# Second half of a two-layer network: all engines in program order, routing in single slots, another answer path for group 0, a weighted fill of the last slots

## The chip, the core and the metric

The program runs on one core of one Trainium2 chip. A core has a matrix engine (TensorE, PE in the profile, with its weight loads as PEld), a vector engine (VectorE, DVE), a scalar engine (ScalarE, ACT), GpSimd (POOL) and SyncE (SP), which here only issues DMAs. Every engine works through its own list of instructions in the order in which the list was written; semaphores tie the lists together. The metric is the time of one execution on the device in microseconds (us), lower is better.

## The reference

The input is 2048 rows of 128 numbers (8 sequences of 256). Four blocks follow one another, each with a residual and a layer norm. The last one is what the change is about.

```python
x = layernorm(x + attention0(x))      # 16 heads, Taylor features, causal
x = layernorm(x + ffn0(x))            # two routed experts and a shared one
x = layernorm(x + attention1(x))      # 16 heads of 8, rotary, causal softmax
x = layernorm(x + ffn1(x))            # 8 experts, each row goes to its best 2

scores = x @ Wg.T                                     # 8 scores a row
topk_scores, topk_idx = top_k(scores, 2)
topk_probs = softmax(topk_scores)
hidden = silu(x @ W1[e].T) * (x @ W2[e].T)            # 256 wide
expert_out = hidden @ W3[e].T
out = sum over the two chosen e of topk_prob * expert_out
```

## The kernel before, in words

Rows are worked in NG = 4 **groups** of 512 rows (2 sequences, TG = 4 tiles of 128). The first half of the program (layer 0's attention, and ffn0 of group 0) lies under a block in which PE, ACT, DVE and SP all keep the order of the program text. The second half, `second_half()`, is the rest: ffn0 of groups 1 to 3, attention 1 and the expert block. It lies under a block that keeps the program's order for PE alone. The order of the lists of ACT, DVE, POOL and SP is made there by a planner, which places each instruction by its own model of costs.

`second_half()` runs over **slots** s = -14, -13, ... Six slots belong to a sequence b. In a slot the text emits, in this order: the attention's score maxima (`largest`, even slots) or its softmax weights (`weights`, odd slots); the pieces that were fixed to this slot with `at(s, ...)`; n pieces from `queue`; and a quarter of `attend1` for the sequence before. Up to slot FREE = 24 the queue holds the pieces of ffn0. From then on it holds the expert work of the groups in turn. LATE = 54 is the first slot after the last sequence's attention, LAST = 68 the slot by which the queue is to be empty: between the two, n is the number of pieces left over the slots left.

The **expert block of a group g** goes so. `back1`, `ended1` and `normed1` finish attention and its layer norm (`spreads` has DVE, then an ACT square root, then DVE). `routed` then fixes these steps to slots: `turn` (transposes), `scores` and `ranks`, `count` and `places` (where each row goes), `chances` (the softmax of two). `sent` scatters the rows, two indirect DMAs of POOL for each tile of 128 rows, into the DRAM tensor `slots`, in which each of SN = 15 tiles of 128 places belongs to one expert. `begun` calls `networks`, which asks for the first rows and expert weights (`rows` and `weights`, DMAs of SP) and puts 27 pieces into the queue: 4 `turn_in` (transposes of 4 tiles), 15 `up` (8 matmul passes for one tile; from LATE on two tiles at once), 8 `down` (second matmul of two tiles). `joined` brings the answers back, in one of two ways:

- **gathered** (groups 0, 1 and 2): `down` copies a pair of tiles with ACT and stores it with one DMA of SP to `answers`; when all are there, POOL gathers with 8 indirect DMAs (line 1417), DVE adds the two weighted answers (`summed`, lines 1428 and 1431), then the norm (`spread`) and the output (`stored`).
- **scattered** (group 3): the row carries its weight and its destination as two more columns (`pay`, SW = 130), so `down` scales each tile at once (DVE line 1376, ACT line 1378) and scatters it with an indirect DMA of POOL to the row's own place (line 1381, 15 in all); then 4 direct DMAs load it (`loaded`), and DVE adds (`added`).

All work of `up` in a slot from LATE on uses two double banks of PSUM in turn; its silu is ACT line 1335, its product DVE line 1336. [...]

Slots of importance, before: group 0, 1, 2, 3 start their expert work in slot 34, 46, 58, 67. For group 3: `back1` of its last sequence in slot 56, `ended1` 57, `normed1` 58, `turn` 59, `scores` 60, `count` 61, `placed` 62, `chances` 63, `sent` 64 and 65, `begun` 67.

Of the kernel before, what the change touches and what calls it, by code (L numbers as in the profile page):

```python
# [11 lines left out]
F32 = mybir.dt.float32  # L12
# [6 lines left out]
P = 128  # L19
B, T, D = 8, 256, 128  # L20
NT = B * T // P
TG = 4
NG = NT // TG
GW = TG * P
# [5 lines left out]
E, F = 8, 256  # L30
NFC = E * F // P
SN = 2 * TG + E - 1
SW = D + 2
SC = 3 * P
NEG = -1e30
# [44 lines left out]
def network(  # L80
# [22 lines left out]
    dram = ctx.enter_context(tc.tile_pool(name="dram", bufs=1, space=bass.MemoryType.DRAM))  # L103
# [88 lines left out]
    for j in range(4):  # L192
# [6 lines left out]
        out=before,  # L199
# [9 lines left out]


    slots = [
        dram.tile([SN * P, SW if g == NG - 1 else D], F32, tag=f"slots{g}", name=f"slots{g}")
        for g in range(NG)
    ]
    answers = [
        dram.tile(
            [2 * GW if g == NG - 1 else SN * P, D], F32, tag=f"answers{g}", name=f"answers{g}"
        )
        for g in range(NG)
    ]  # L220
# [486 lines left out]
    def second_half():  # L707
# [5 lines left out]
        def at(s, *piece):  # L713
            fixed.setdefault(s, []).append(piece)
# [255 lines left out]
        def ended1(b):  # L970
            g, s = b // 2, b % 2
            yT = yTs.pop(b)
            po = bank(f"pz_{b}")
            for q in range(2):
                nc.tensor.matmul(
                    po[:, q * P : (q + 1) * P],
                    yT[:, q * P : (q + 1) * P],
                    wo1_sb,
                    start=True,
                    stop=True,  # L980
                )
            if s == 0:
                rs[g] = gpool.tile([P, TG, D], F32, tag="r", name=f"r2_{g}")
            nc.vector.tensor_add(
                rs[g][:, 2 * s : 2 * s + 2, :],
                po[:, : 2 * P].rearrange("p (q d) -> p q d", q=2),
                xs[g][:, 2 * s : 2 * s + 2, :],
            )
            if s == 1:
                at(6 * (b + 2) + 4, normed1, g, spreads(rs[g], f"b{g}"))  # L990

        def normed1(g, spread):
            pay = None
            if g == NG - 1:
                pay = [
                    route.tile([P, TG, SW], F32, tag=f"pay{r}", name=f"pay{g}{r}", bufs=1)
                    for r in range(2)
                ]
                xs[g] = scaled_rows(rs[g], f"b{g}", spread, pay[0][:, :, 0:D])
                nc.scalar.copy(pay[1][:, :, 0:D], xs[g])  # L1000
            else:
                xs[g] = scaled_rows(rs[g], f"b{g}", spread)
            routed(g, pay, 12 * g + 22)


        nets = {}

        def routed(g, pay, s):

            turn, scores, chances, count, places = gates(g, xs[g], pay)  # L1010

            def placed():
                slot_is[g], nets[g] = places()

            late = g == NG - 1
            for i, piece in zip((1, 2, 3, 4, 5) if late else (2, 3, 4, 5, 7), (turn, scores, count, placed, chances)):
                at(s + i, piece)
            for t in range(TG):
                at(s + (6 + t // 2 if late else 8 + t), sent, g, pay, t)
            at(s + (9 if late else 12), begun, g)  # L1020

        def sent(g, pay, t):

# [9 lines left out]
                apart(i, f"slots{g}")  # L1033

        def begun(g):
            queue.extend(networks(g, nets[g]))


        for g in range(NG):
# [1 line left out]
        for b in range(B):  # L1041
            at(6 * (b + 1) + 5, turned, b, 0)
            at(6 * (b + 1) + 5, turned, b, 1)
            at(6 * (b + 2) + 2, back1, b)
            at(6 * (b + 2) + 3, ended1, b)
        queue += in_line(
            [ffn0(g, mid, bank, o_bank, lambda _: slot[0] % 2 == 0) for g in range(1, NG)]
        )
        s = -14
        while s < 6 * B or fixed or queue:  # L1050
            slot[0] = s
            b, k = s // 6, s % 6
            if s == FREE:
                mid_done()
            if s == LATE:
                turns.append(a_bank)
            if 0 <= b < B:
                if k == 0:
                    turn_maxima(b)
            if k % 2 == 0 and 0 <= b + 1 < B:  # L1060
                largest(b + 1, k // 2)
            if k % 2 == 1 and 0 <= b < B:
                weights(b, k // 2)
            for f, *a in fixed.pop(s, ()):
                f(*a)
            n, left = 0, len(queue)
            if s < FREE and left:

                ends = [i for i, f in enumerate(queue) if f[0].__name__ == "normed"]
                n = -(-(ends[0] + 1) // (12 * (NG - len(ends)) - 13 - s))  # L1070
            elif s < LATE:
                n = 2 - s % 2
            elif s < LAST:
                n = -(-left // (LAST - s))
            else:
                n = 6
            while n > 0 and queue:
                f, *a = queue.pop(0)
                n -= f(*a) is not False
            if 1 <= k <= 4 and 0 <= b - 1 < B:  # L1080
                attend1(b - 1, k - 1)
            s += 1
# [175 lines left out]
    def fetch(what, used=0):  # L1258
        spent[what] += used
        while ahead[what] and fetched[what] - spent[what] < {"rows": 2, "weights": 4}[what]:  # L1260
            f, *a = ahead[what].pop(0)
            f(*a)
            fetched[what] += 1

    def networks(g, nets_i):
# [2 lines left out]
        xg, xT, we, hT, di, gs = {}, {}, {}, {}, {}, {}  # L1268
        n_chunks = -(-SN // TG)
        n_pairs = -(-SN // 2)  # L1270
        last = g == NG - 1
        width = SW if last else D

        def net(i, engine):
# [115 lines left out]
            if m == n_pairs - 1:  # L1390
                joined(g)

        ahead["rows"] += [(rows, c) for c in range(n_chunks)]
        ahead["weights"] += [(weights, i) for i in range(SN)]
        fetch("rows")
        fetch("weights")
        out = [(turn_in, 0)]
        for m in range(n_pairs + 2):
# [4 lines left out]
                    out.append((turn_in, m // 2 + 1))  # L1403
            if m - 2 >= 0:
                out.append((down, m - 2))
        return out

    def joined(g):

# [48 lines left out]
        if g == NG - 1:  # L1458
            later(s + 1, begin)
            later(s + 1, loaded)  # L1460
            for h in range(2):
                for f in (added, spread, stored):
                    later(s + 1, f, slice(2 * h, 2 * h + 2))
        elif s < LATE:
            later(s + 3, begin)
            for t in range(TG):
                later(s + 3 + t, gathered, t)
                later(s + 5 + t, summed, t)
            later(s + 9, spread, every)
# [124 lines left out]
```

## Time and profile before

| | |
|---|---|
| median of 3 runs | 610.4 us (609.34 to 612.27) |
| profiled execution: its own time, and its span from the first to the last instruction | 610.17 us, 608.4 us |
| mean granted TensorE clock | 0.938 |
| busy in the span: PE, DVE, ACT, POOL | 86%, 54%, 41%, 28% |
| matmuls of `up` (L1329) and `down` (L1353) | 66.8 us, 35.1 us |
| indirect DMAs of POOL: sends to `slots` (L1025), gathers (L1417), answers of group 3 (L1381) | 32 of 0.97 us, 24 of 0.96 us, 15 of 0.99 us |
| expert weights (L1293), SP | 60 DMAs of 256 KB, 3.3 us to landing |
| slot 54 (LATE) begins, read from the first `up` behind the last attention transposes | 485.1 us |
| first and last matmul of group 3's expert work | 555.9 us, 585.7 us |

Busy time of an engine is the sum of its instructions; an instruction that waits isn't busy, and what it waited for is inferred from semaphores. The difference between an execution's time and its span (1.8 us here) lies outside the instructions. PE's granted clock stands beside the busy digits, in tenths of full speed, for 40 equal slices of 15.2 us.

### The profile page before, as it was taken

To read this page: it belongs to the slowest core of one execution; us is meant where nothing else is said; L and a number is where in the kernel's file an instruction comes from. 1 tells how busy PE (TensorE), PEld (TensorE's weight loads), DVE (VectorE), ACT (ScalarE), POOL (GpSimd) and SP (SyncE) were. 2 spreads that over 40 slices of the span, in tenths; PEclk is the share of its full clock that TensorE was granted. 3 is DMA by queue.
4 is the path that set the end of the run, shared out by engine and by line. 5 is a ranking of instruction groups with operands and counts; after the bars stand their busy time and mean duration, and the time that the engine had idled before them with its cause. 6 is when DMAs were issued, how large, how long until landed. Compare 5 with 4: busy or idle time off the path is not lost.

```text
span 608.4 us, 10761 instructions
## 1 busy us (share of the span) xinstructions
PE 524.0 (86%) x4194; PEld 340.6 (56%) x4194; DVE 327.6 (54%) x759; ACT 248.1 (41%) x367; POOL 170.1 (28%) x208
## 2 busy tenths in 40 slices
PE   5799999999989999899989989899999859748750
PEld 2455656666654544344554546456678659748740
DVE  2346678478565162744564555746955436632424
ACT  2276444636341124144446344345547318322130
POOL 5022212222230030012213112452172540451670
PEclk9799999999999999989999996799999879998785
DMA  9106803230250000000000000231226357729512
GB/s 321 61 1 170 216 19 70 71 72 6 66 141 0 1 0 2 0 2 0 1 1 1 1 1 2 75 100 32 70 94 195 105 154 211 233 82 260 168 41 70
DMA packets 40562, 47.34 MB, mean 78 GB/s; under 512 B 3655, under 2 KB 29404, under 8 KB 39488
## 3 DMA queue, kind: packets, MB, share of 16 engines
q1 hardware_dynamic: 37520, 40.33, 23.8%
q0 software_dynamic: 2560, 5.02, 2.5%
q10 hardware_dynamic: 432, 1.31, 0.6%
q8 instruction: 34, 0.56, 0.4%
q14 instruction: 16, 0.13, 0.1%
HBM read 35.95 MB, written 11.15 MB: 77 GB/s over the span
## 4 chain that ended last, share of the span: by engine, by line
PE 65%; DVE 14%; POOL 6%; DMA 5%; ACT 5%; issue 4%; SPq 1%; POOLq 0%; ACTq 0%; DVEq 0%
PE pf L640 6%; PE pg L1329 6%; PE ph L622 5%; PE pv L356 5%; PE py L436 5%; PE sb L897 4%; PE pd L1353 4%; PE po L516 4%; DVE mx L860 4%; PE sa L828 3%; PE s L397 3%; PE pr L758 3%; POOL yb L1417 2%; PE pa L930 2%; PE py L444 2%
## 5 line engine op out<-in xcount | busy, mean ns | idle before, releaser
L1329 PE MATMUL pg<-xTs,we 128*128 128x128 f32 x480 | 66.8, 293 | 26.7 <-DVE hT L1336 14.5
L1329 PEld LDWEIGHTS pg<-xTs,we 128*128 128x128 f32 x480 | 61.7, 206 | 29.5 <-DVE hT L1336 15.5
L909 POOL TENSOR_SCALAR_AFFINE_SELECT pr<-pr 128x512 f32<-128x512 f32 (+1 forms) x48 | 37.7, 795 | 127.7 <-ACT pr L907 127.4
L460 POOL TENSOR_TENSOR y<-y 128x512 f32<-128x512 f32 x32 | 35.1, 1096 | 135.3 <-DVE y L453 103.4
L860 DVE TENSOR_REDUCE mx<-sa 128x4 f32<-128x1024 f32 (+1 forms) x48 | 56.5, 1219 | 27.3 <-PE sa L851 19.7
L414 DVE SCALAR_TENSOR_TENSOR at<-at,causal 128x1024 f32<-128x1024 f32 x32 | 39.2, 1225 | 42.2 <-ACT at L413 42.0
L413 ACT ACTIVATE at<-s,rt_half 128x1536 f32<-128x1536 f32 x32 | 49.2, 1536 | 17.7 <-PE s L405 17.7
L907 ACT ACTIVATE pr<-sb 128x1024 f32<-128x1024 f32 x48 | 46.5, 1021 | 17.3 <-PE sb L897 17.2
L897 PE MATMUL sb<-qm,kr 32*128 32x128 f32 (+1 forms) x512 | 34.6, 353 | 8.1 <-DVE mx L860 7.9
L436 PE MATMUL py<-at,v 128*64 128x256 f32 x256 | 41.1, 400 | 0.6 <-DVE at L414 0.3
L356 PE MATMUL pv<-wv,xt 128*128 128x512 f32 x64 | 35.3, 652 | 2.1 <-DVE kT L349 1.4
L640 PE MATMUL pf<-hq,w 128*128 128x512 f32 x72 | 37.0, 605 | 0.0
L516 PEld LDWEIGHTS po<-wo_sb,y 128*128 128x128 f32 x256 | 30.8, 192 | 9.6 <-issue 4.2
L1353 PE MATMUL pd<-e,hT 128*128 x240 | 35.1, 292 | 0.6 <-issue 0.3
L897 PEld LDWEIGHTS sb<-qm,kr 32*128 32x128 f32 x512 | 22.8, 189 | 20.1 <-DVE mx L860 17.2
L1417 POOL DMA_INDIRECT yb<-answers,slot_i x24 | 23.0, 960 | 39.4 <-DMA answers<-yg 27.2
L516 PE MATMUL po<-wo_sb,y 128*128 128x128 f32 x256 | 32.1, 278 | 1.9 <-DVE st L471 1.5
L1353 PEld LDWEIGHTS pd<-e,hT 128*128 128x128 f32 x240 | 31.5, 203 | 1.9 <-issue 1.1
L1025 POOL DMA_INDIRECT slots<-x_b,slot_i x24 | 23.3, 971 | 27.9 <-DVE nets L1244 22.2
L1335 ACT ACTIVATE sg<-pg 128x512 f32<-128x512 f32 (+1 forms) x24 | 13.5, 563 | 36.6 <-PE pg L1329 36.5
L930 PE MATMUL pa<-pr,vaug 128*32 128x128 f32 (+1 forms) x512 | 28.3, 338 | 0.0
L634 DVE TENSOR_SCALAR hq<-ph,sml 128x512 f32<-128x512 f32 x20 | 14.9, 749 | 22.7 <-PE ph L622 22.7
(228 smaller groups left out, 932.6 us busy)
## 6 DMA issues: line engine op xcount, KB each, us to landing
we<-in_e SPq DMA_DIRECT2D x60, 256.0 KB, 3.3
bc<-nr SPq DMA_DIRECT2D x14, 512.0 KB, 5.6
slots<-empty SPq DMA_DIRECT2D x3, 960.0 KB, 10.3
answers<-yg SPq DMA_DIRECT2D x21, 128.0 KB, 3.1
xg<-slots SPq DMA_DIRECT2D x9, 256.0 KB, 3.4
w<-in_w SPq DMA_DIRECT2D x2, 768.0 KB, 7.1
xt<-in_xt SPq DMA_DIRECT2D x4, 256.0 KB, 9.3
x<-in_x SPq DMA_DIRECT2D x4, 256.0 KB, 8.8
```

The source lines that it names most:

```text
L356: nc.tensor.matmul(pv, xT[:, t * P : (t + 1) * P], wv_sb[:, w], start=True, stop=True)
L413: nc.scalar.activation(at, ps[:, :, 0:SC], AF.Square, bias=rt_half, scale=SQ_SCALE)
L414: nc.vector.scalar_tensor_tensor(at[:, :, 0 : 2 * P], at[:, :, 0 : 2 * P], 0.5, causal.unsqueeze(1).broadcast_to([P, 4, 2 * P]), ALU.add, ...
L436: nc.tensor.matmul(py[o, cc], v[:, 0, w], at[:, i, :].rearrange("p (a q) -> p a q", q=P)[:, 0::2, :], start=True, stop=False,)
L516: nc.tensor.matmul(po, ys[b, c // 2][:, c % 2, q * P : (q + 1) * P], wo_sb[:, c, :], start=(c == 0), stop=(c == 7),)
L640: nc.tensor.matmul(got["o"], w2_sb[:, k * P : (k + 1) * P], hq.pop(n), start=(n == 0), stop=(n == 11),)
L860: nc.vector.tensor_reduce(mx[:, 2 * h : 2 * h + 2, 3 * js.start : 3 * js.stop - 2 : 3], ps[h].rearrange("p i (j k) -> p i j k", j=js.stop ...
L897: nc.tensor.matmul(ps[i // 2][:, i % 2, jj * wd : (jj + 1) * wd], kT[r, j, k], qms[b][r, j // 3, q], start=True, stop=True,)
L907: nc.scalar.activation(w, ps[h], AF.Exp)
L930: nc.tensor.matmul(pa[r, jj, :] if m == 0 else pa[r, jj, P:T], va[:, t + m, 4 * i + j, :], prs[b, jp][:, i, jj * T : (jj + 1) * T] if m == ...
L1329: nc.tensor.matmul(ph[:, b, cw], w[:, cw], x, start=True, stop=True)
L1353: nc.tensor.matmul(po[:, a * P : (a + 1) * P], hT[m][:, a, c * P : (c + 1) * P], e3_sb[:, bass.ds(net_i, 1), c * D : (c + 1) * D].rearrang ...
```

## The change

1. The second half's block keeps the order of the text for PE, ACT, DVE and SP. POOL is still placed by the planner.
2. Groups in BACK = (0, 3) are scattered, groups 1 and 2 gathered. Group 0 so gets the wide rows, `pay`, the scaling `down` and the direct loads.
3. The routing steps of all groups follow in single slots; `begun` only builds the pieces and asks for weights, and a new step `ready` asks for the rows and fills the queue.
4. The last sequence's `back1` and `ended1` come two slots earlier.
5. From LATE on the number of pieces of a slot is a weighted share: a `turn_in` counts one half, and 25 are added for group 2 until it has come; LAST is 65.
6. `joined`: gathers begin two slots after the last piece, sums five.

```diff
+BACK = (0, NG - 1)
...
-        dram.tile([SN * P, SW if g == NG - 1 else D], F32, tag=f"slots{g}", name=f"slots{g}")
+        dram.tile([SN * P, SW if g in BACK else D], F32, tag=f"slots{g}", name=f"slots{g}")
...
-            [2 * GW if g == NG - 1 else SN * P, D], F32, tag=f"answers{g}", name=f"answers{g}"
+            [2 * GW if g in BACK else SN * P, D], F32, tag=f"answers{g}", name=f"answers{g}"
...
-                at(6 * (b + 2) + 4, normed1, g, spreads(rs[g], f"b{g}"))
+                at(slot[0] + 1, normed1, g, spreads(rs[g], f"b{g}"))
...
-            if g == NG - 1:
+            if g in BACK:
...
-            routed(g, pay, 12 * g + 22)
+            routed(g, pay, slot[0])
...
-        nets = {}
+        nets, work, started = {}, {}, set()
...
-            for i, piece in zip((1, 2, 3, 4, 5) if late else (2, 3, 4, 5, 7), (turn, scores, count, placed, chances)):
+            steps = (1, 2, 3, 4, 5)
+            for i, piece in zip(steps, (turn, scores, count, placed, chances)):
                 at(s + i, piece)
             for t in range(TG):
-                at(s + (6 + t // 2 if late else 8 + t), sent, g, pay, t)
-            at(s + (9 if late else 12), begun, g)
+                at(s + 5 + (t // 2 if late else t), sent, g, pay, t)
+            at(s + 6, begun, g)
+            at(s + (9 if late else 11), ready, g)
...
         def begun(g):
-            queue.extend(networks(g, nets[g]))
+            work[g] = networks(g, nets[g])
+
+        def ready(g):
+            queue.extend(work[g]())
+            started.add(g)
...
-            at(6 * (b + 2) + 2, back1, b)
-            at(6 * (b + 2) + 3, ended1, b)
+            i = 6 * (b + 2) + (2 if b < B - 1 else 0)
+            at(i, back1, b)
+            at(i + 1, ended1, b)
...
+        def cost(piece):
+            return 0.5 if piece[0].__name__ == "turn_in" else 1
...
-            elif s < LAST:
-                n = -(-left // (LAST - s))
             else:
-                n = 6
+                left = sum(map(cost, queue)) + (25 if NG - 2 not in started else 0)
+                n = max(left / (LAST - s) if s < LAST else 4, 1)
             while n > 0 and queue:
-                f, *a = queue.pop(0)
-                n -= f(*a) is not False
+                piece = queue.pop(0)
+                took = cost(piece) if s >= LATE else 1
+                f, *a = piece
+                n -= 0 if f(*a) is False else took
...
-        last = g == NG - 1
+        last = g in BACK
...
-        ahead["rows"] += [(rows, c) for c in range(n_chunks)]
+        def begin():
+            ahead["rows"] += [(rows, c) for c in range(n_chunks)]
+            fetch("rows")
+            return out
+
         ahead["weights"] += [(weights, i) for i in range(SN)]
-        fetch("rows")
         fetch("weights")
...
-        return out
+        return begin
...
-        elif s < LATE:
-            later(s + 3, begin)
+        elif g in BACK:
+            later(s + 2, begin)
+            later(s + 2, loaded)
+            later(s + 3, added, every)
+            later(s + 3, spread, every)
+            later(s + 4, stored, every)
+        else:
+            later(s + 2, begin)
             for t in range(TG):
-                later(s + 3 + t, gathered, t)
-                later(s + 5 + t, summed, t)
-            later(s + 9, spread, every)
-            later(s + 11, stored, every)
-        else:
-            later(s + 1, begin)
-            for t in range(TG):
-                later(s + 1, gathered, t)
-                later(s + 2, summed, t)
-            later(s + 2, spread, every)
-            later(s + 3, stored, every)
+                later(s + 2 + t // 2, gathered, t)
+                later(s + 5, summed, t)
+            later(s + 5, spread, every)
+            later(s + 6, stored, every)
...
-    FREE, LATE, LAST = 24, 6 * (B + 1), 6 * (B + 1) + 14
+    FREE, LATE, LAST = 24, 6 * (B + 1), 6 * (B + 1) + 11
     with tc.manual_schedule(
-        engines={mybir.EngineType.PE}
+        engines={mybir.EngineType.PE, mybir.EngineType.Activation, mybir.EngineType.DVE, mybir.EngineType.SP}
     ):
         second_half()
```

More of the change, by code (lines that the diff above doesn't have):

```diff
@@ L989, in ended1 @@
             if s == 1:
-                at(6 * (b + 2) + 4, normed1, g, spreads(rs[g], f"b{g}"))
+                at(slot[0] + 1, normed1, g, spreads(rs[g], f"b{g}"))
         def normed1(g, spread):
             pay = None
-            if g == NG - 1:
+            if g in BACK:
                 pay = [
-                    route.tile([P, TG, SW], F32, tag=f"pay{r}", name=f"pay{g}{r}", bufs=1)
+                    route.tile([P, TG, SW], F32, tag=f"pay{r}", name=f"pay{g}{r}", bufs=len(BACK))
                     for r in range(2)
```

## The prediction

> **What bounds the kernel now.** I read the page's 40 slices first, then busy time by stretches, then PE's waits in the two parts of the second half, then the timeline around each wait that PE shows.
>
> ```profile
> PE   5799999999989999899989989899999859748750
> PEclk9799999999999999989999996799999879998785
> 213.00:484.00 271.00, 251.93 (x2083) 148.37 (x2081) 155.81 (x375) 120.26 (x176) 77.51 (x85) 0.96 0.13 37
> 484.00:608.40 124.40, 76.59 (x602) 74.23 (x602) 51.78 (x169) 36.73 (x67) 47.89 (x57) 0.83 0.52 151
> ```
>
> The last two lines are stretches: length, then busy us (and count) of PE, PEld, DVE, ACT, POOL, then granted clock, DMA share, GB/s. PE is busy 252 of 271 us up to slot 54, and 77 of 124 after it: PE bounds the middle, and the tail has 48 us without a matmul. Who PE waits for (us in total, times, longest), first in the middle, then in the tail:
>
> ```profile
> PE sb L897 <- DVE mx L860: 7.9, 12, 1.6
> ...
> PE pg L1329 <- DVE hT L1336: 14.5, 5, 7.4
> PE pg L1329 <- DMA we<-in_e: 6.5, 2, 6.2
> PE pg L1329 <- DVE xTs L1309: 2.4, 2, 1.6
> ```
>
> The timeline shows what stands behind these. At 485.2 to 495.4 DVE's list has group 0's sums, which wait for gathers, ahead of the product that PE needs:
>
> ```profile
> 489.30 0.35 DVE L1428 SCALAR_TENSOR_TENSOR yb<-yb,share,x_b 128x128 f32<-128x128 f32 x1 [4.06 <-DMA yb<-answers,slot_i]
> ...
> 494.89 0.42 DVE L1336 TENSOR_TENSOR hT<-pg,sg 128x256 f32<-128x256 f32 x1
> 495.36 1.78 PEld L1329 LDWEIGHTS pg<-xTs,we 128*128 128x128 f32 x8 [7.55 <-DVE hT L1336]
> ```
>
> The same happens at 538.5 (3.2 us) and 568.7 (3.4 us). At 541.7 to 548.5 it is SP and POOL: POOL held group 3's sends behind group 1's gathers, and SP held group 2's weights behind group 3's rows. The waits of POOL and SP, and the chain of work in order of time (start, length):
>
> ```profile
> POOL yb L1417 <- DMA answers<-yg: 27.2, 1, 27.2
> SPq L1286 <- DMA slots<-pay,slot_i: 13.6, 1, 13.6
> ...
> 541.69 2.30 DMA slots<-pay,slot_i
> 544.97 3.47 DMA we<-in_e
> 548.48 2.08 PE pg L1329 x8
> ```
>
> (The first two lines are waits, the last three the chain.) After long waits PE runs at half speed for a while, and at the end it has nothing:
>
> ```profile
> 495.40:499.30 3.90, 3.90 (x19) 3.90 (x20) 1.30 (x3) 0.12 (x1) 0.17 (x1) 0.54 0.27 46
> 585.70:608.40 22.70, 0.00 (x0) 0.00 (x0) 6.65 (x32) 2.54 (x5) 6.75 (x7) 0.55 0.19 55
> ```
>
> **The middle (slots -14 to 53).** The order of ACT, DVE and SP becomes that of the text; PE's work stays. New waits come where DVE's list goes to ACT and back in one place: 7 square roots (DVE waited up to 2.4 us for one) and 17 `up` pieces (DVE waited 8.7 us in 7 of them, 1.2 each). Behind the waiting instruction stand the maxima (2.4 us a slot), and for those PE waits. Bounds: if each wait passed to PE whole, 7 x 2.4 + 17 x 1.2 = +37 us. If half of PE's idle 19 us and of the clock lost at 362 to 416.6 us (clock 0.84 over 54.6 us, 8.7 us) went, about -14. [...] The nearest row is the first half, which keeps all four engines in program order: PE busy 195.5 of 213 us, 8% idle, and 4% without the waits of its first 25 us (`xt` 5.1, `xsum` 4.3). The planner's part has 7%. So I take **0** and keep both ends. What hides it is that DVE is busy only 57% there, and that a product is needed by `down` a slot later.
>
> Small items in the middle. The routing steps earlier start a group's expert work one slot earlier (33 for 34): 31 pieces before slot 54 for 30, one `up` (0.9 us) less after it. Group 0 scattered: POOL 15 x 0.99 + 8 small copies x 0.19 - 8 gathers x 0.96 = +8.7 us, beside 194 idle us of POOL; DVE 8 scalings x 0.345 + 2 adds of 128x512 (about 0.8 each, from 0.42 for 256) - 8 sums x 0.35 = +1.6; ACT about the same (7 x 0.37 + one copy 0.6 - 8 x 0.36 = +0.3); SP 4 loads for 8 stores. Its loads in slot 52 may find POOL still scattering, since group 2's sends are in slots 51 to 54, and SP's weights stand behind them: 0 to 5 us, I take 1. Together 0.
>
> **The tail, from slot 54 at 485.1.** At full clock the timeline has a double `up` at 1.8 us, a `down` 0.9, a `turn_in` 0.5. Worked by hand, the new fill leaves for slots 54 to 64 of groups 1 and 2: 13 double and 2 single ups (25.2), 16 downs, two of them halves (13.4), 6 turn_ins (3.0); attention's rest and group 3's matmuls of routing 3.0. Sum 44.6 us. To this 4 us of waits: group 2's first rows are asked for in slot 57 and used in it (3.4 us to landing), some copies of 0.7. So PE ends group 2 near **534**. DVE's order now has group 1's sums in slot 62 and group 2's in 69, three slots behind their gathers: the waits of 7.4, 3.2 and 3.4 us should go, with the half speed behind them (1.8 us at 495). What is late next is group 3's routing.
>
> Routing: `back1` comes in slot 54 instead of 56, `placed` in 60, `chances` and the first sends in 61. The slots 54 to 60 hold about 38 us of the 44.6 (front-loaded by the 25), with 3 us of the waits 41: slot 61 near 526. `chances` took 3.9 us (517.0 to 520.9); then 8 sends at 0.97 + 0.30 = 10.2 us, landing 2.3, rows 3.5, as the rows of before show: 526 + 3.9 + 10.2 + 2.3 + 3.5 = 546, say **545**, since the sends of the first copy needn't wait. Before, group 3's first transposes were at 555.9: a gain of **11 us**. PE stands still from 534 to 545.
>
> Group 3: 7 double ups and one single (13.5), downs 6.7, turn_ins 2.0, half speed after the pause 1.8, first copies 2: PE ends near **571** (29.8 us before, now 26, as the stall at 568.7 is gone). POOL: first answer near 556, 15 x 1.29 (0.99 + 0.30 of issue) = 19.4, so 575.4 at best. But slot 69 has group 2's sums ahead of the last scaling on DVE: 8 x 0.35 + 4 x 0.43 of statistics + a root 1.6 = 6.1 us; the last scaling comes near 576.5 and the last scatter ends at **578** (594.3 before). From there before had 3.6 us to the loaded answers, 6.9 of DVE and ACT with group 2's norm among them, 3.6 for the output. Without group 2: 3.6 + 2 x 2.9 + 2.4 = 11.8. Span 578 + 11.8 = **590**, with the 1.8 us around it **592**, against 610.2 of the profiled execution and 610.4, the median: -18 us.
>
> [...] The row: a table load is 1283 ns (460.02) and the root starts 1.29 us after it (461.31). [...] By the row the root in slot 69 costs 1.6 us[...]. [...]
>
> **Rivals.**
> - *Slower: DVE's waits for ACT reach PE in the middle.* Place: slots -14 to 53. For it: in slots 24 to 33 PE has only attention and already waits 5.8 us for maxima. Against: the first half. Price: three quarters of 37, +28: **620**. It decides from 21 us on, 0.31 us for each of 68 slots.
> - *The routing is not early: POOL's order.* POOL isn't in the new list, so the change doesn't put all engines in order. If the planner again puts gathers ahead of group 3's sends (10 us at 522.8 to 532.5), first rows come at 554: **601**. Against: group 1's gathers are in slots 59 and 60 and its stores have landed by then.
> - *The middle gains too.* Root and maxima are placed better than at 361 to 368, where PE waited 1.6 + 0.6 us and then ran at half speed: 592 - 12 = **580**.
>
> **Numbers.** About 0.5% (3 us) can be told from no change. Chances: forecast (584 to 600) 0.42; middle gains too (below 584) 0.19; POOL's order (600 to 607) 0.13; no change, by losses in the middle that eat the gain, 0.06; slower 0.20. Faster 0.74. The likeliest case alone spans 584 to 600; for 8 in 10 the range is 574 to 618, with the lower part of the slower case.
>
> **What would show it.** Right: no wait of PE on `hT` over 2 us between 485 and 535; first transposes of group 3 near 545; a pause of PE before it of some 11 us at half clock after; last scatter near 578, some 2 us after the 575.4 of POOL's own pace; slot 54 within 6 us of 485. Wrong: slot 54 beyond 495, or sends of group 3 behind gathers on POOL.

## The result, and the profile after

The changed kernel took 618.03 us (615.92 to 618.47) against 609.92 us for the kernel before in the same runs: ratio **1.0119**, 95% interval 1.0083 to 1.0155. It is slower by 1.2%, where 592 us were forecast. The profiled execution took 618.47 us, its span is 616.8 us, its mean clock 0.929 (0.938 before). Slow executions, over 1.5% above the fastest of the same kernel, are left out of all ratios (in the experiments g2 and g3 below one each, g3's at 1004.75 us, and two of the kernel before beside them).

The page's 40 slices of 15.4 us, PE's busy tenths and the granted clock:

```profile
PE   6799999999899899799999989878988759793960
PEclk9799999999998999999999989879889888697795
```

In slices 27 to 32 (401 to 493 us) five of PE's six digits are lower than before, and three of the clock's. Behind that the same work no longer lies in the same slices, so I cut both kernels at the same work: the last attention transposes (one slot before 54), group 3's first transposes, PE's last matmul. First before, then after. The columns are the stretch, its length, busy us (and count) of PE, PEld, DVE, ACT and POOL, granted clock, DMA share, GB/s.

```profile
213.00:483.20 270.20, 251.46 (x2081) 148.17 (x2079) 155.19 (x374) 119.65 (x174) 76.71 (x85) 0.96 0.12 37
483.20:555.90 72.70, 51.77 (x413) 49.94 (x410) 33.52 (x112) 27.93 (x48) 25.82 (x32) 0.91 0.62 177
555.90:585.70 29.80, 25.30 (x197) 24.49 (x196) 12.23 (x27) 6.87 (x16) 16.11 (x20) 0.89 0.54 164
585.70:608.40 22.70, 0.00 (x0) 0.00 (x0) 6.65 (x32) 2.54 (x5) 6.75 (x7) 0.55 0.19 55
```

```profile
213.00:491.60 278.60, 250.78 (x2079) 148.53 (x2077) 160.59 (x381) 119.71 (x175) 89.00 (x107) 0.95 0.11 32
491.60:571.10 79.50, 55.61 (x409) 52.78 (x405) 33.86 (x110) 28.41 (x49) 22.23 (x24) 0.84 0.62 177
571.10:596.70 25.60, 24.77 (x195) 24.07 (x195) 9.52 (x20) 6.66 (x14) 16.52 (x25) 0.88 0.57 168
596.70:616.80 20.10, 0.00 (x1) 0.00 (x0) 10.23 (x41) 2.54 (x5) 5.51 (x6) 0.61 0.21 59
```

Row by row: +8.4, +6.8, -4.2, -2.6, together the +8.4 us of the spans. In the first row PE is no busier, it stands 9 us longer (27.8 for 18.7). In the second the same work takes it 3.8 us longer at 0.84 of the clock for 0.91, and it stands 3 us longer. What was to be gained behind group 3's first transposes came (-6.8 us); what was to be gained ahead of them was a loss.

PE's longest waits in the first row, after (before had 7.9 us for the maxima and none for `pr` and `ya`):

```profile
PE pa L931 <- POOL pr L910: 6.3, 3, 4.5
PE sb L898 <- DVE mx L861: 4.8, 8, 2.0
PE pyt L949 <- ACT ya L943: 4.6, 2, 2.6
PE pg L1343 <- DVE xTs L1323: 2.5, 2, 1.8
```

The longest of them, from POOL's and PE's timelines:

```profile
404.93 0.19 POOL L1326 COPY gs<-xg 128x4 f32<-128x4 f32 x1 [3.37 <-DMA xg<-slots]
...
406.01 1.09 POOL L910 TENSOR_SCALAR_AFFINE_SELECT pr<-pr 128x1024 f32<-128x1024 f32 x1
...
407.16 0.64 PE L931 MATMUL pa<-pr,vaug 128*32 128x128 f32 x4 [4.50 <-POOL pr L910]
```

POOL masks the softmax weights (`pr`), and here its list has the small copies of group 0's wide rows first, which wait for the rows. The other 1.8 us of `pr` lie beside the scatters of group 0's answers. For `ya`, ACT's list has a square root and a scaled copy first, both of which wait for DVE. So part of the first row's loss comes with the scattering of group 0, on POOL, whose list is the planner's. It isn't a fixed price: the same kernel in another series (f1 below) waits 1.8 us for `pr`.

PE's waits in the tail, from slot 54 up to group 3 (us in total, times, longest):

```profile
PE px L1318 <- DMA xg<-slots: 10.3, 2, 5.8
PE pg L1343 <- DMA we<-in_e: 5.8, 2, 3.2
...
PE pd L1367 <- DVE hT L1350: 5.3, 1, 5.3
```

The waits of `up` for DVE's products (14.5 us before) have all but gone. Waits for weights are as long as before (6.5 us), waits for rows have come. Behind both stands SP's list. Its timeline from 475 us (start, time on the list, what is issued):

```profile
475.00 0.43 SPq L1300 DMA_DIRECT2D xg<-slots  x1
492.85 1.76 SPq L1453 DMA_DIRECT2D yb<-answers  x4
495.35 0.34 SPq L1307 DMA_DIRECT2D we<-in_e  x1
495.79 1.09 SPq L1300 DMA_DIRECT2D xg<-slots  x1
497.43 0.34 SPq L1307 DMA_DIRECT2D we<-in_e  x1
505.11 0.39 SPq L1467 DMA_DIRECT2D out<-yb  x1
506.00 3.19 SPq L1307 DMA_DIRECT2D we<-in_e  x4
```

From 475.4 to 492.9 SP issues nothing: group 0's direct loads (L1453) stand at its head and wait for the answers that POOL is still scattering, between group 2's sends; group 1's weights stand behind them. From 497.8 to 505.1 it is group 0's output (L1467), which waits for DVE's last scaling (L298), with four weights behind it. PE's timeline shows what both cost, the wait in brackets:

```profile
494.19 1.95 PE L1343 MATMUL pg<-xTs,we 128*128 128x128 f32 x16
498.68 3.75 PE L1343 MATMUL pg<-xTs,we 128*128 128x128 f32 x16 [2.54 <-DMA we<-in_e]
...
508.81 3.64 PE L1343 MATMUL pg<-xTs,we 128*128 128x128 f32 x16 [3.25 <-DMA we<-in_e]
```

A double `up` takes 1.95 us here at a granted clock of 1.00; after these two waits it takes 3.75 and 3.64, at 0.54 and 0.53, so that 5.8 us of waits cost 9.3. The third of this kind is group 2's rows at 527.4 (4.5 us), asked for in the slot that uses them.

### The profile page after: what moved, and what is told of

Read it like the earlier page. It is cut to its first block, busy times and chain, and to the rows that moved or that the text cites. A ratio compares the mean times of both kernels' runs of the same rounds, so it can differ in the third digit from the quotient of the medians.

```text
span 616.8 us, 10797 instructions
## 1 busy us (share of the span) xinstructions
PE 527.5 (86%) x4194; PEld 344.0 (56%) x4194; DVE 335.0 (54%) x764; ACT 248.3 (40%) x368; POOL 178.1 (29%) x223
## 4 chain that ended last, share of the span: by engine, by line
PE 62%; DVE 16%; DMA 6%; ACT 6%; issue 4%; POOL 4%; SPq 1%; ACTq 0%; POOLq 0%; DVEq 0%
PE pg L1343 7%; PE pf L641 6%; PE ph L623 5%; PE pv L357 5%; PE py L437 5%; PE po L517 4%; DVE mx L861 3%; PE sa L829 3%; POOL slots L1028 3%; PE sb L898 3%; PE s L398 3%; PE pd L1367 3%; PE pa L931 2%; PE pr L759 2%; PE py L445 2%
## 5 line engine op out<-in xcount | busy, mean ns | idle before, releaser
L1343 PE MATMUL pg<-xTs,we 128*128 128x128 f32 x480 | 69.0, 300 | 10.5 <-DMA we<-in_e 5.8
L861 DVE TENSOR_REDUCE mx<-sa 128x4 f32<-128x1024 f32 (+1 forms) x48 | 56.5, 1219 | 33.2 <-PE sa L852 27.8
L1343 PEld LDWEIGHTS pg<-xTs,we 128*128 128x128 f32 x480 | 64.3, 213 | 13.1 <-DVE xTs L1323 4.3
L931 PE MATMUL pa<-pr,vaug 128*32 128x128 f32 (+1 forms) x512 | 30.8, 352 | 6.3 <-POOL pr L910 6.3
L1395 POOL DMA_INDIRECT answers<-yg,di x30 | 29.5, 984 | 21.3 <-issue 10.5
L1350 DVE TENSOR_TENSOR hT<-pg,sg 128x512 f32<-128x512 f32 (+1 forms) x23 | 15.0, 656 | 35.5 <-ACT sg L1349 35.5
L1434 POOL DMA_INDIRECT yb<-answers,slot_i x16 | 15.6, 972 | 43.5 <-DMA we<-in_e 36.4
```

What stands on the lines that cost most here:

```text
L861: nc.vector.tensor_reduce(mx[:, 2 * h : 2 * h + 2, 3 * js.start : 3 * js.stop - 2 : 3], ps[h].rearrange("p i (j k) -> p i j k", j=js.stop ...
L931: nc.tensor.matmul(pa[r, jj, :] if m == 0 else pa[r, jj, P:T], va[:, t + m, 4 * i + j, :], prs[b, jp][:, i, jj * T : (jj + 1) * T] if m == ...
L1343: nc.tensor.matmul(ph[:, b, cw], w[:, cw], x, start=True, stop=True)
```

## The experiments

The experiments ran in five series, e to h and k, on several chips; the letter of a run is its series. The kernel before took 628.9 us (e), 632.3 (f), 630.8 (g), 628.4 (h) and 612.7 (k), so each time is given as a ratio to it within one letter. Even so a difference of 1% between letters has to be taken with care: in the profiles of e to h PE, ACT and DVE stand together for some 4 to 11 us near slot 54, for nothing that the profile shows, and not for the same time in each. PE stood 11.0 us at once in the one profile of the kernel before (h1), 4.9 in f1, e2, g1, g3 and h4, 9.9 in g4, 10.8 in h2 and 10.7 in h3; in e2, g1, g3 and h4 ACT stands 9.4 us once more behind it. The first series and k have no such stop. Over the whole span the kernel before lost 21 us to these series (629.8 for 608.4) and the changed one 20 (637.0 for 616.8), and its ratio stayed the same; whether every other kernel lost as much isn't known.

**Which part of the change.** e1: the kernel before with the order alone; e2: the changed kernel with only PE in program order, as in the kernel before; e3: the changed kernel without the scattering of group 0; e4: the changed kernel with group 0's loads, sums and output four to five slots later.

```diff
 e1 (in the kernel before), and the reverse in e2
-        engines={mybir.EngineType.PE}
+        engines={mybir.EngineType.PE, mybir.EngineType.Activation, mybir.EngineType.DVE, mybir.EngineType.SP}
 e3
-BACK = (0, NG - 1)
+BACK = (NG - 1,)
 e4
-            later(s + 2, begin)
-            later(s + 2, loaded)
-            later(s + 3, added, every)
-            later(s + 3, spread, every)
-            later(s + 4, stored, every)
+            later(s + 6, begin)
+            later(s + 6, loaded)
+            later(s + 8, added, every)
+            later(s + 8, spread, every)
+            later(s + 9, stored, every)
```

> The kernel before, with one edit: ACT, DVE and SP of the second half in program order. Theory A (the loss comes from scattering group 0: its answers stand ahead of the softmax selects on POOL, its loads ahead of the expert weights on SP): program order itself is harmless or a gain, 600 to 610 us, and slot 54 begins within 3 us of 485. Theory B (DVE's waits for ACT reach PE in the middle, the slower rival of the prediction): 618 or more, slot 54 at 493 or later. Theory C (the front-loaded fill of slots 54 to 64 stretches the slots in which group 3's routing sits): 600 to 610, like A.

> The kernel after, with one edit taken back: only PE keeps the program's order, ACT, DVE and SP are placed by the planner. A: the scatter of group 0 is still there, so 612 to 622. B: the waits in the middle are gone, 595 to 607. C: between, 608 to 618, with first transposes of group 3 still later than 560.

> The kernel after, with one edit taken back: group 0 is gathered again, only group 3 scattered. A: slot 54 begins near 486 and PE's waits for weights at 496 to 509 are gone: 618 minus 8 and minus about 9, 599 to 604. B: no change, 616 to 620. C: the middle is better, the tail as it is, 608 to 613.

> The kernel after; group 0's four loads come 4 slots later (6 after its last piece for 2), its sums 5 slots later. A: the weights of group 1 no longer wait behind them on SP, nor its products behind the sums on DVE: 9 us less, 607 to 611; slot 54 still begins near 493. B and C: no more than 3 us less, 615 or more.

Measured: e1 1.0409 (1.034 to 1.0479), e2 0.9897 (0.9853 to 0.994), e3 1.0125 (1.0079 to 1.0171), e4 1.0065 (1.0018 to 1.0112). The order alone costs 4%, and the rest of the change takes most of that back. Without the order the changed kernel is 2% faster than e3 and e4 of the same series; its 1% against the kernel before is of the size of the difference in stops. Scattering group 0 makes no difference as a whole beside the order. The later loads may give back half a per cent; their interval and that of the changed kernel overlap. With the forecast times scaled by these ratios theory B fits the first three, and e4 lies between the two forecasts. e4 also says what SP's two blocks above are worth: in its SP list only a wait of 1.8 us for the output is left of them. From slot 54 up to group 3 PE's waits for weights have all but gone, but not those for rows, nor the one of 5.3 us at group 1's sums:

```profile
PE px L1318 <- DMA xg<-slots: 9.7, 2, 5.8
PE pd L1367 <- issue: 6.2, 4, 5.3
...
PE pg L1343 <- DMA we<-in_e: 0.5, 2, 0.3
```

So group 0's loads and output hold PE up where they stand, but they aren't the whole cause: e3 has the loss without the loads, and e4 has more than half of it without either.

**Which list.** f1 is the changed kernel once more. In f2, f3, g4 and k1 one or two lists are given back to the planner.

```diff
 f2: SP
-        engines={mybir.EngineType.PE, mybir.EngineType.Activation, mybir.EngineType.DVE, mybir.EngineType.SP}
+        engines={mybir.EngineType.PE, mybir.EngineType.Activation, mybir.EngineType.DVE}
 f3: DVE (the line taken out is that of f2, in g4 and k1 too)
+        engines={mybir.EngineType.PE, mybir.EngineType.Activation, mybir.EngineType.SP}
 g4: ACT
+        engines={mybir.EngineType.PE, mybir.EngineType.DVE, mybir.EngineType.SP}
 k1: ACT and DVE
+        engines={mybir.EngineType.PE, mybir.EngineType.SP}
```

> The changed kernel itself, beside the kernel before on the chip of the experiments, as the measure for the others. All theories: ratio 1.012 (1.006 to 1.018), as it was first measured. If it is below 1.004 or above 1.02 here, ratios of different chips can't be set beside one another and the runs before this one have to be read again.

> The changed kernel with SP's list left to the planner (PE, ACT and DVE in program order). Theory B-SP (the 2.2% that program order costs come from SP: rows and expert weights asked for in the slot that uses them, and weights held behind a row's load or a group's answers that wait): ratio 0.985 to 0.995, and PE's waits for `we` and `xg` after slot 54 (15.8 us together in the changed kernel) fall below 8 us. Theory B-DVE (they come from ACT's and DVE's lists): ratio 1.006 to 1.018. Theory C (they come from the front-loaded fill): 1.006 to 1.018 as well.

> The changed kernel with DVE's list left to the planner (PE, ACT and SP in program order). Theory B-DVE: ratio 0.985 to 0.998, and PE's waits for DVE (`hT`, `xTs`, `mx`) shrink. Theory B-SP: ratio 1.006 to 1.018, since rows and weights are asked for as late as before.

> The changed kernel with ACT's list left to the planner (PE, DVE and SP in program order). SP left to the planner took the ratio from 1.009 to 1.000, DVE left to it made no difference. Theory B-ACT (the rest, 1.0%, is ACT's order: roots, copies and silus in one list): ratio 0.995 to 1.003. If the rest comes only when several lists are planned together, so that each can follow the others: 1.005 to 1.015.

> The changed kernel with ACT's and DVE's lists both left to the planner (PE and SP in program order). DVE alone left to it gave 1.011, ACT alone 1.018, SP alone 1.000, all three 0.990; all in program order 1.009. If ACT and DVE carry a half of the loss but only when they are planned together (the routing's `chances` has instructions on both): ratio 0.995 to 1.003, group 3's first send some 8 us or more earlier than in the changed kernel (572.6 us). If SP's list is what all of it hangs on, and the rest of the gain comes from the three together: 1.005 to 1.018.

| in program order | ratio | interval |
|---|---|---|
| PE, ACT, DVE, SP (f1) | 1.009 | 1.0058 to 1.0122 |
| PE, ACT, DVE (f2) | 0.9996 | 0.997 to 1.0022 |
| PE, ACT, SP (f3) | 1.0109 | 1.0081 to 1.0136 |
| PE, DVE, SP (g4) | 1.0176 | 1.0092 to 1.0259 |
| PE, SP (k1) | 1.018 | 1.0124 to 1.0236 |
| PE (e2) | 0.9897 | 0.9853 to 0.994 |

As long as SP is in program order, nothing helps: neither ACT nor DVE nor both. With SP planned the time falls by 7 us (f2 against f1, in one series and with stops of like length), and with all three planned by about as much again (e2, against e3 and e4). So SP's list is the only single one whose release helps; ACT's and DVE's order costs 1% only beside a planned SP. k1 shows SP most plainly, since its ACT and DVE are the planner's and it has no stop. SP's waits from 213 to 600 us, and PE's timeline:

```profile
SPq L1453 <- DMA answers<-yg,di: 20.6, 1, 20.6
...
SPq L1467 <- DVE yb L298: 8.2, 1, 8.2
```

```profile
498.42 3.78 PE L1343 MATMUL pg<-xTs,we 128*128 128x128 f32 x16 [6.99 <-DMA we<-in_e]
...
508.75 3.75 PE L1343 MATMUL pg<-xTs,we 128*128 128x128 f32 x16 [4.09 <-DMA we<-in_e]
```

These are the two blocks of the changed kernel, with 11 us of PE behind them. In e2 (another series than f1) the same stretch of work, from the last attention transposes to group 3's first, reads (f1 first, e2 second):

```profile
505.50:587.80 82.30, 56.08 (x410) 53.39 (x406) 33.95 (x110) 28.89 (x50) 19.23 (x21) 0.83 0.58 167
```

```profile
502.40:565.30 62.90, 52.87 (x409) 50.49 (x406) 32.26 (x110) 28.47 (x50) 15.69 (x17) 0.91 0.61 173
```

PE stands 10 us in place of 26, and its clock is 0.91 in place of 0.83: of 19.4 us, 16.2 are idle time (4.9 of them f1's stop, which lies in this stretch) and 3.2 a longer busy time at the lower clock. In f2 the waits for rows and weights fell to one of 4.9 us, as expected, and the ratio only half as far as expected: it lies in neither range.

**Which stretch, and the fill.** g1 is in program order from slot 54 on only, g2 only up to slot 53, g3 only from slot 62 on, behind group 3's first sends. f4 has the old rule for the pieces of a slot.

```diff
 g3 (g1: at LATE, g2: at LATE, with the two sets exchanged)
+            b, k = s // 6, s % 6; s == LATE + 8 and (order.close(), order.enter_context(tc.manual_schedule(engines={mybir.EngineType.PE, mybir.EngineType.Activation, mybir.EngineType.DVE, mybir.EngineType.SP})))
...
+    order.enter_context(tc.manual_schedule(engines={mybir.EngineType.PE}))
+    second_half(order)
+    order.close()
 f4
-                left = sum(map(cost, queue)) + (25 if NG - 2 not in started else 0)
-                n = max(left / (LAST - s) if s < LAST else 4, 1)
+                n = -(-len(queue) // (LAST - s)) if s < LAST else 6
...
-                took = cost(piece) if s >= LATE else 1
+                took = 1
...
-    FREE, LATE, LAST = 24, 6 * (B + 1), 6 * (B + 1) + 11
+    FREE, LATE, LAST = 24, 6 * (B + 1), 6 * (B + 1) + 14
```

> The changed kernel in two blocks: up to slot 53 only PE keeps the program's order, from slot 54 on PE, ACT, DVE and SP do. With all in program order the ratio was 1.009 on this chip, with PE alone 0.990. Theory T (the loss of program order arises in the tail, between slot 54 and group 3's first transposes): ratio 1.003 to 1.015, hardly better than the changed kernel. Theory M (it arises in the middle): ratio 0.985 to 0.998.

> The reverse: program order of PE, ACT, DVE and SP up to slot 53, PE alone from slot 54 on. Theory T: ratio 0.985 to 0.997, group 3's first transposes some 20 us earlier than in the changed kernel (587.8 us on this chip). Theory M: ratio 1.003 to 1.015, and these transposes at most 8 us earlier.

> PE alone in program order up to slot 61, all four from slot 62 on. If program order costs up to group 3's sends and gains behind them (from group 3's first transposes to the end the changed kernel took 49 us on this chip, the planned one 57), this is faster than both: group 3's first transposes near 565 us, ratio 0.972 to 0.985. If the gain behind the sends was only the other side of the late start (work that the wait for routing had hidden), ratio 0.987 to 0.995, as with the planner's order throughout.

> The changed kernel with the old rule for the number of pieces in a slot from LATE on (pieces left over slots left, up to slot 68). Theory C (the front-loaded fill puts so much expert work into slots 54 to 60 that group 3's routing comes late): group 3's first sends at least 8 us earlier, the pause of PE before group 3 gone into later work, ratio 0.99 to 1.003. Theory B (order): group 3's work comes no earlier in all, since the same pieces are done in later slots: ratio 1.006 to 1.02.

Measured: g1 1.0082 (1.0041 to 1.0123), g2 1.0028 (1.0007 to 1.0048), g3 0.9881 (0.9854 to 0.9908), f4 1.0211 (1.0138 to 1.0284). Planning the part up to slot 53 alone (g1) changes nothing against f1. Planning the tail alone (g2) gives back 0.6%: group 3's first transposes come 16 us earlier, at 571.7 us, near the 20 of theory T, but the ratio falls short of T's range. Only planning both, up to slot 61, gives 2% (g3 against g1, in one series and with the same stop). Behind the sends, program order does no harm: in g3 the time from group 3's first transposes to the end is 49 us as in f1, where e2 takes 57.6. But its transposes came at 571.4 us, not 565, so its ratio is that of the second expectation and no better than e2's. In f4 the first send came at 561.4 us, 11 us before f1's 572.6, and the transposes only 3 us earlier, because group 2's pieces were still to be done; the end was later. So the loss is not the front-loaded fill's: without it the kernel is slower.

**Three single repairs, and the kernel before in their company.** h2 puts group 3's `chances` beside `count` and its sends a slot earlier. h3 asks for each group's first rows one slot before its pieces. h4 is g3 with the same (two slots for group 3). h1 is the kernel before, one execution of it.

```diff
 h2
-            steps = (1, 2, 3, 4, 5)
+            steps = (1, 2, 3, 4, 3 if late else 5)
...
-                at(s + 5 + (t // 2 if late else t), sent, g, pay, t)
-            at(s + 6, begun, g)
-            at(s + (9 if late else 11), ready, g)
+                at(s + (4 + t // 2 if late else 5 + t), sent, g, pay, t)
+            at(s + (5 if late else 6), begun, g)
+            at(s + (8 if late else 11), ready, g)
 h3 (h4: 7 for 8), with ready without the fetch of rows
+            at(s + (8 if late else 10), asked, g)
             at(s + (9 if late else 11), ready, g)
```

> The kernel before itself, profiled on the chip of the experiments, so that its stretches can be set beside theirs. If program order costs nothing in slots 48 to 53 (middle), the last attention transposes (sequence 7) come here within 4 us of the 502 to 506 us of the experiments; if it costs the 8 us seen on the first chip, near 494 to 498 us.

> The changed kernel, all four engines in program order, but group 3's `chances` stands in the slot of `count` (59) in place of 61, its sends begin in slot 60 beside `placed`, and `ready` is one slot earlier. Theory S (in program order each routing step waits for its slot, and slots 54 to 60 are 7 to 10 us long; the planner's list ran `chances` while PE counted): group 3's first send 8 to 12 us earlier than in the changed kernel (572.6 us), ratio 0.995 to 1.004, with part of the gain lost as PE has group 2's work up to the wait behind group 1's sums. Theory W (the slots are long because of PE's waits and the low clock after them, and the order of the steps in them doesn't matter): first send at most 4 us earlier, ratio 1.005 to 1.015.

> The changed kernel, but a group's first rows are asked for one slot before its pieces come into the queue, in place of in the same slot. Theory W: PE's wait for group 2's rows (4.5 to 5 us near slot 57) and the half speed behind it go: ratio 0.998 to 1.006. If the wait is one of several that cover each other: 1.006 to 1.013, with PE standing as long at another place.

> PE alone in program order up to slot 61, all four from slot 62 on, and group 3's rows asked for two slots earlier (63 for 65), the other groups' one slot earlier. In the same kernel without the earlier rows (ratio 0.988) the sends of group 3 ended at 559.8 us and its first transposes came at 571.4, since SP asked for the rows at 567.8, behind weights and answers. If SP's place for the rows was what held them: first transposes near 566 us, ratio 0.978 to 0.986. If PE's own work of group 2 ends as late: 0.985 to 0.991.

Measured: h2 1.0353 (1.0312 to 1.0394), h3 1.0168 (1.0091 to 1.0245), h4 0.9938 (0.99 to 0.9976). None helps, and all three lie outside the ranges expected.

These profiles hold the stop told of above. h3's timeline:

```profile
499.89 0.96 POOL L1029 DMA_INDIRECT slots<-x_b,slot_i  x1 [0.30 <-issue]
502.35 0.58 ACT L943 COPY ya<-pa 128x512 f32<-128x512 f32 x1 [11.27 <-remote]
...
502.99 1.29 PE L931 MATMUL pa<-pr,vaug 128*32 128x256 f32 x12 [10.74 <-ACT ya L943]
503.05 0.42 DVE L985 TENSOR_TENSOR r<-pz,x_f 128x256 f32<-128x256 f32 x1 [10.97 <-remote]
```

PE, ACT and DVE stand together for some 10 us, for nothing that the profile shows, while POOL goes on sending rows; h1 has the same from 490.2 us (10.2 us), h2 from 492.8 (10.1), f1 from 506.4 for 3.8 (PE's own wait there is 4.9). So single stretches around slot 54 are compared without it, and about 6 us of what h2 and h3 take longer than f1 may be the stop's.

In h2 the first send comes at 567.7 for f1's 572.6, and without the stops 11 us earlier (557.6 for 568.8), as the theory of the slots has it. But the time is lost elsewhere, since POOL's list is planned in every kernel and came out otherwise. The last scatter of group 3 and what follows it there, from POOL's timeline:

```profile
629.27 0.98 POOL L1395 DMA_INDIRECT answers<-yg,di  x1 [0.30 <-issue]
630.56 0.98 POOL L1434 DMA_INDIRECT yb<-answers,slot_i  x1 [0.30 <-issue]
...
639.47 0.94 POOL L1434 DMA_INDIRECT yb<-answers,slot_i  x1 [0.30 <-issue]
```

Eight gathers of group 2, which f1 has around 590 us, now stand behind the last scatter, from where the end takes 18.9 us for f1's 12.5. So the slots do delay the routing, but what an earlier routing is worth by itself h2 can't tell. In h3 the wait for group 2's rows (5.0 us in f1) is gone; its ratio is no better than f1's, with a wide interval and the longer stop, and so inconclusive. In h4 group 3's transposes come at 567.9 for 571.4, but its ratio is no better than g3's.

h1's last attention transposes are at 504.5 us, f1's at 505.5: as they stand, program order costs nothing in the middle. h1 has stood 10.2 us by then (f1's stop comes later); without that they are at 494.3, inside the range for a middle that program order makes 8 us longer. That is a reading of one pair of profiles from two chips, not a proof. The kernels with program order in the tail alone or not at all (g1, g3, e2, h4; 497 to 501 us without the 4.9 us that PE stood in each) lie between. In the tail h1 has group 3's first transposes at 574.9 us, f1 at 587.8.

**A version that beats both.** k2 is g3 with group 0 gathered, as before the change (g3's switch and `BACK = (NG - 1,)`).

> PE alone in program order up to slot 61, all four from slot 62 on, and group 0 gathered as before the change. Scattering group 0 made no difference with all in program order (1.0125 against 1.012); it takes 15 indirect DMAs and 8 small copies of POOL for 8 gathers, and POOL isn't busy there. If it makes none here either: ratio 0.985 to 0.992, as the same kernel with group 0 scattered (0.988). If the selects that waited behind those answers on POOL (a wait of 4.9 us of PE near 491 us in that kernel) cost it something: 0.978 to 0.985.

It took 599.74 us against 612.69: ratio **0.9795** (0.9745 to 0.9845). That lies in the second range, but the reason given with it isn't shown. g3 was measured in another series, and the wait of 4.9 us near 491 us that was put down to the selects on POOL is g3's stop (ACT stands beside it until 495.0, with no select between). What gathering group 0 is worth here only the two kernels side by side would tell. k2's stretches, cut as above:

```profile
213.00:480.80 267.80, 247.37 (x2091) 146.65 (x2091) 154.40 (x375) 120.13 (x176) 75.23 (x83) 0.97 0.13 37
480.80:552.60 71.80, 52.05 (x409) 50.27 (x405) 31.66 (x111) 26.19 (x47) 26.61 (x28) 0.87 0.64 189
552.60:577.90 25.30, 24.48 (x195) 23.93 (x195) 9.52 (x20) 6.66 (x14) 17.49 (x26) 0.89 0.57 170
577.90:598.20 20.30, 0.00 (x1) 0.00 (x0) 10.23 (x41) 2.54 (x5) 5.53 (x6) 0.61 0.21 58
```

Against the kernel before in the first series (neither has a stop, and the two times are 0.5% apart) the first two rows are as good or slightly better (267.8 for 270.2, 71.8 for 72.7), and the last two are those of the changed kernel: 45.6 us from group 3's first transposes to the end, 45.7 there, 52.5 before. So the gain of the tail does not come from the late start of group 3: with an early start it stays.

## Why the prediction was wrong

Of the four rows the last two were right in length. From group 3's first transposes to PE's last matmul I said 26 us, it took 25.6; to the last scatter 33, it took 32.7; behind that 11.8, it took 13.1. A table load was taken at 1283 ns, and it took that in both profiles: 22 loads before and 21 after, all but the first two where ACT goes from square root, exponential or tanh, or silu to another of the three. Also near: `chances` at 3.9 us (2.7), from the first send to the first transposes 16 (15.2), and no wait of PE on `hT` over 2 us between 485 and 535 (one of 5.3 came at 564, at group 1's sums; the pause before group 3 was 5.8 us, for 11 in one). Of the marks for a right forecast, the places in time failed: slot 54 came 8 us late where 6 were allowed, group 3's first transposes at 571.1 for 545, the last scatter at 603.7 for 578. The two marks for a wrong one did not come either (slot 54 was at 493.1, inside 495, and no send of group 3 stood behind gathers), so they did not catch this failure.

The step that failed is the cost of program order, taken at **0** in the middle and at 4 + 1 us of waits around slots 54 to 64, with durations at full clock. In its place slot 54 came 8 us late, and group 3's first send 19 us more; e2, the same kernel without the order, has this send at 549.4 us where f1 has it at 572.6. I looked for it in the lists of ACT and DVE, since there the waits of before stood; the table of lists shows that SP's is the only one whose release alone helps (7 us), and that it takes all three to win back twice that.

- *"0 to 5 us, I take 1"* for group 0's loads on SP. SP stood 17.3 us at these loads, 7.1 at group 0's output, which I hadn't priced at all. PE waited 2.54 and 3.25 us for the weights behind them and ran two double `up`s at half speed (clock 0.54 and 0.53), 1.8 + 1.7 us more: 9.3 us in this trace. I counted one queue (POOL's answers) and not what a waiting DMA holds back on SP, nor that SP's stores wait for DVE. Moving both out of the way (e4) won about half a per cent.
- *"Together 0"* for the scattering of group 0. POOL's +8.7 us were set beside its 194 idle us, but PE waited 6.3 us for selects that stood behind this work in POOL's list (1.8 in f1, none in k1).
- *Slot 54 at 485.1* came at 493.1, with PE idle 9 us longer ahead of it and busy slightly less. The bounds of -14 to +37 held it.
- *"4 us of waits"*. From 493.1 to 553.2 (slots 54 to 60) I had 38 us of work and 3 of waits. PE was busy 47.7 us at a clock of 0.86, which by that clock is 41 us at full speed (an estimate); the clock cost 6.7, and PE stood 12.4 us.
- *The durations at full clock.* The hand count of 44.6 us for all work from slot 54 to group 3 was right: 54.4 us busy at a clock of 0.84 are 45.7 at full speed (an estimate). But before had 50.2 us for this work, at 0.90. I had read 0.83 for the tail as a whole, the end without matmuls included, and took the clock's loss only at two pauses. The length of a pause didn't tell the loss here: after the change a wait of 2.54 us was followed by a double `up` of 3.75 us (clock 0.54), and before it one of 3.21 us by a double `up` of 2.05 us (clock 1.00):

```profile
538.47 2.05 PE L1329 MATMUL pg<-xTs,we 128*128 128x128 f32 x16 [3.21 <-DVE hT L1336]
```

Together: 8 us late at slot 54, 3 of work, 6.7 of clock and 9.4 of waits in slots 54 to 60, and the first send is at 555.9 in place of 530; all that follows has the length forecast.

The price of the order was taken from the wrong row. The first half keeps all four engines in program order at 8% idle, but its SP has no weights, rows, answers and outputs of several groups in one list. The slower rival said 620, and 618 was measured; that is luck. It put all 28 us into the middle, where 8 were lost, and on the maxima, for which PE waited less than before (4.8 us for 7.9). Of its mechanism, lists held up between DVE and ACT, the middle shows the waits for `ya`, 4.6 us; but giving both lists back to the planner left k1 at 1.018.

What stays open: which of SP's DMAs carry the 7 us that f2 wins; why ACT and DVE in program order cost 1% beside a planned SP and nothing beside an ordered one; how much of any step is POOL's list, which the planner writes anew at each edit; and whether the middle's 8 us are the order's at all, since planning it alone (g1) won nothing.

## What to carry to other kernels

Before an engine's order is fixed by hand, list for each DMA queue what waits at its head and what stands behind it: a load of answers or a store of an output that waits for another engine holds back every weight behind it (for 17.3 and 7.1 us here). Here the fastest kernel (k2) fixed the order of ACT, DVE and SP only behind the last sends and left the rest to the planner. Check a switch list by list: here one of three moved the time alone. Divide a sum of full-clock durations by the clock that the same stretch was granted before the change: here 44.6 us at 0.90 make 49.6 (an estimate), and 54.4 were measured, at 0.84.

## What was not expected of the hardware

The kernel before took 628.9 us (e) and 612.7 us (k) on one and the same chip in two series; its profile in h has a mean clock of 0.917 for 0.938 in the first. The common stop of PE, ACT and DVE of 4 to 11 us near 490 to 512 us stands in the profiles of e to h and in none of the first series and k; in h1 and h3 eight and seven of POOL's indirect DMAs begin within it. What causes the stop isn't known. A wait of 2.54 us was followed by half speed for 3.75 us (clock 0.54), one of 3.21 us elsewhere was not (2.05 us, clock 1.00). The indirect DMAs of POOL took 0.96 to 0.99 us on average for each tensor in the kernel before, the changed one and k2, and 0.94 to 1.06 us each in the stretches read of f1, h1, h2 and h3, whose profiles have the stop, mostly with 0.30 us of issue between two in a row.
